# A graph-convolution and Mamba kernel: gate products moved to GpSimd, reductions joined, B's parts split elsewhere, weights loaded between the first rows, last pass on 128 partitions

## The chip, the cores and the metric

The kernel runs on one core of a Trainium2 chip. The core has TensorE (PE) for matmuls, VectorE (DVE), ScalarE (ACT) and GpSimd (POOL) for elementwise work, and SyncE (SP), whose queue issues most of the DMAs here. Each engine works through its own list of instructions in order and waits for others by semaphores. The metric is the time of one execution on the device, in microseconds (us), as the median of the runs.

## The reference, cut to what matters

The input `x` is 16 images of 96 channels and 64 x 64 pixels. A first layer builds a graph inside each 8 x 8 window and takes a maximum over edges; a second runs two Mamba layers over the 4096 pixels of an image and normalises over the whole batch.

```python
# layer 0
y = affine(conv1x1(x, fc1_w, fc1_b), fc1_s, fc1_t)
nodes = windows of 8 x 8 of y                      # 64 nodes of 96 channels
idx = top_k(-dist(nodes), 9)                       # nearest nodes, the node itself among them
feat = concat(x_i, x_j - x_i)                      # per edge, 192 values
h = gelu((einsum('bnkc,oc->bnko', feat, ew) + eb) * es + et)
h = max(h, over the 9 edges)                       # 192 channels
x = affine(conv1x1(h, fc2_w, fc2_b), fc2_s, fc2_t) + x
# layer 1, twice (D = 192 channels, 16 states)
xs, z = split(layernorm(seq) @ in_w)
xc = silu(causal_conv4(xs))
dt, Bm, Cm = split(xc @ xproj_w)                   # 6, 16, 16 columns
delta = softplus(dt @ dt_w + dt_b)
hstates = scan of h = exp(delta * A) * h + delta * Bm * xc
y = einsum(hstates, Cm) + Dp * xc
seq = seq + (y * silu(z)) @ out_w                  # the gate product
# then
out = fus_w @ concat(seq, relu(mean(x) @ gp_w))
out = batchnorm(out) * bn_g + bn_b + x
```

All inputs and outputs are float32.

## The kernel before, in words

**Tiling.** A *row* is 512 pixels (8 image rows, 8 windows) of one image: 128 rows. An *item* is a row in one of the two Mamba layers: 256 items, in the order image, layer, row. The 192 channels of Mamba lie on 128 partitions as 512 + 256 columns (the last 64 channels are folded over two halves), and in the scan as 128 partitions (two states of 64 channels each) by 3 groups by 512 pixels. So the 16 states of an item take 8 *steps*, and the loop has 2048 steps.

**The loop** (`for m, (n, p) in enumerate(order)`). In a step, VectorE scans `hb` from `da` and `db` (L861), then multiplies `u` by B's broadcast row into the next `db` (L707); in most items a small add (L852) carries the state over from the row before. PE makes the broadcast row from `bparts` with a 0/1 matrix (`bcast`, L702). ScalarE makes `da = exp(delta * A)` (L681) two steps ahead. GpSimd multiplies `hb` by C's rows `ct` (L887), which SyncE brings from DRAM (L674). One step later PE adds that product into `y` with `fold` (`folded`, L715 to L720). At step 1 of the next item VectorE multiplies `y`, in PSUM, into `z` (`gates`, two instructions issued at L850 or L854), and at step 6 `tail` projects the result (L740 to L745).

**Beside the steps** generators run, each advanced by one `yield` per step: `norm` and `prelude` for item n + 2 (they make `xc`, `z`, B, C, `delta`, `u`), `carry`, and layer 0 of a later row, one per two items: `nearest` (distances and the eight nearest, with `max` and `max_index` on VectorE) and `edges` (one-hot matrices, matmuls, Gelu into a `da` tile in groups of three, maxima over 8 edges). The maxima are queued: `later` holds them for two steps, `between` hands out at most one before the scan and one in steps 4 and 5 behind it, and `late` empties the rest. Yields marked TABLE keep `exp` away while another activation table is loaded. `apart`, `open_steps` and `close_steps` put a product at the end of a step and its use at the start of the next.

**B's parts.** bparts holds B three times in bfloat16, so that the three parts add up to float32. `xproj` yields B in three row groups; ScalarE casts all of them (L613) and casts a remainder again (L647), GpSimd subtracts twice over 512 columns (L640, L657).

**Head and end.** All weights are loaded and prepared first, mostly by ScalarE's queue (`compact`, `rows`, and the setup loop L195 to L254). Then `drain` runs `nearest` for rows 0 to 7 and `edges` for rows 0 to 5, one row's `nearest` beside the `edges` of the row before, then `norm` and `prelude` of items 0 and 1 one after another; the loop begins. The last pass (L908 to L918) waits for the statistics of all rows, reads `o_d` and `x1_d` in tiles of 96 x 2048, applies scale and shift, adds and writes.

Of the kernel before, what the change touches and what calls it, by code (L numbers as in the profile page):

```python
# [10 lines left out]
F32 = mybir.dt.float32  # L11
# [10 lines left out]
def tile_conv_knn_mamba(ctx: ExitStack, tc: tile.TileContext, w: dict, out: bass.AP):  # L22
# [85 lines left out]
    def compact(name, src):  # L108

        t = const.tile([128, 2], F32, name=name)  # L110
        src = src.rearrange("(p o) -> p o", o=1)
        nc.scalar.dma_start(out=t[:, 0:1], in_=src[:128])
        for h in range(2):
            nc.scalar.dma_start(out=t[h * CB : (h + 1) * CB, 1:2], in_=src[128:])
        return t

    def rows(name, src, n, pool=const):


        t = pool.tile([128, 3, n], F32, name=name)  # L120
        nc.vector.memset(t, 0.0)
        nc.scalar.dma_start(out=t[:, 0, :], in_=src[:128])
        for h in range(2):
            nc.scalar.dma_start(out=t[h * CB : (h + 1) * CB, 1 + h, :], in_=src[128:])
        return t
# [4 lines left out]
    e_b, e_s, e_t = (compact(f"e{k}", w[f"L0_conv_e{k}"]) for k in "bst")  # L130
    fc2T = rows("fc2T", w["L0_conv_fc2_w"], C)
# [28 lines left out]
    PARTS = (0, 64, 96)  # L160
    ONE0 = PARTS[2] + NS
# [14 lines left out]
    das = [const.tile([128, NB3, Q], F32, name=f"da{i}") for i in range(NDA)]  # L176
    zeros = const.tile([128, NB3], F32, name="zeros")
# [15 lines left out]
    conv_in, z_in, conv_b, xproj, dt_w, a_neg, dp_diag, out_w = ([] for _ in range(8))  # L193
    with tc.tile_pool(name="setup", bufs=2) as sp, tc.tile_pool(name="setup_ps", bufs=2, space=PSUM) as spp:
        for i in range(NL):  # L195


            iw = sp.tile([C, 2 * D], F32, tag="iw", name=f"in_w{i}")
            nc.scalar.dma_start(out=iw, in_=w["L1_conv_in_w"][i])
            g = sp.tile([C, 1], F32, tag="g", name=f"g{i}")  # L200
            nc.scalar.dma_start(out=g, in_=w["L1_conv_ln_g"][i].rearrange("(p o) -> p o", o=1))
            lb = sp.tile([C, C + 1], F32, tag="lb", name=f"lb{i}")
            nc.vector.memset(lb, 0.0)
            nc.scalar.dma_start(out=lb[:, C : C + 1], in_=w["L1_conv_ln_b"][i].rearrange("(p o) -> p o", o=1))
            gw = sp.tile([C, 2 * D], F32, tag="gw", name=f"gw{i}")
            nc.vector.tensor_scalar(gw, iw, g, None, ALU.mult)
            cm = sp.tile([C, C + 1], F32, tag="cm", name=f"cm{i}")
            nc.vector.memset(cm, 0.0)
            nc.vector.tensor_copy(cm[:, :C], cmat)
            pb = spp.tile([C + 1, 2 * D], F32, tag="pb", name=f"pb{i}")  # L210
            nc.tensor.matmul(pb, lhsT=cm, rhs=gw, start=True, stop=False)
            nc.tensor.matmul(pb, lhsT=lb, rhs=iw, start=False, stop=True)
            wz = const.tile([128, D], F32, name=f"z_in{i}")
            nc.vector.memset(wz, 0.0)
            nc.vector.tensor_copy(wz[: C + 1], pb[:, D:])
            z_in.append(wz)
            cw = sp.tile([C + 1, NT, D], F32, tag="cw", name=f"cw{i}")
            nc.scalar.dma_start(
                out=cw.rearrange("p k d -> p (k d)"),
                in_=w["L1_conv_conv_w"][i].rearrange("k d -> (k d)").unsqueeze(0).to_broadcast([C + 1, NT * D]),  # L220
            )
            wc = const.tile([128, NT, D], F32, name=f"conv_in{i}")
            nc.vector.memset(wc, 0.0)
            nc.vector.tensor_tensor(wc[: C + 1], cw, pb[:, :D].unsqueeze(1).to_broadcast([C + 1, NT, D]), ALU.mult)
            conv_in.append(wc)

            conv_b.append(compact(f"conv_b{i}", w["L1_conv_conv_b"][i]))
            xr = rows(f"xr{i}", w["L1_conv_xproj_w"][i], R + 2 * NS, sp)
            xp = const.tile([128, 3, ONE0], F32, name=f"xproj{i}")
            nc.vector.memset(xp, 0.0)  # L230
            for r, src, n in ((0, R, 2 * NS), (DT0, 0, R), (PARTS[1], R, NS), (PARTS[2], R, NS)):
                nc.vector.tensor_copy(xp[:, :, r : r + n], xr[:, :, src : src + n])
            xproj.append(xp)
            out_w.append(rows(f"out_w{i}", w["L1_conv_out_w"][i], C))
            dw = const.tile([128, D], F32, name=f"dt_w{i}")
            nc.vector.memset(dw, 0.0)
            nc.scalar.dma_start(out=dw[DT0 : DT0 + R], in_=w["L1_conv_dt_w"][i])
            nc.scalar.dma_start(out=dw[ONE0 : ONE0 + 1], in_=w["L1_conv_dt_b"][i].rearrange("(o d) -> o d", o=1))
            dt_w.append(dw)
            an = const.tile([128, NB3, NPR], F32, name=f"a{i}")  # L240
            for k in range(NB3):
                for h in range(2):
                    nc.scalar.dma_start(
# [136 lines left out]
    def most(out, g, at):  # L380

        nc.vector.tensor_reduce(out, g, AX.X, ALU.max)  # L382
        if at is not None:
            free.append(at)
# [560 lines left out]
```

## Time and profile before

| what | us |
|---|---|
| median of three runs (13182.12, 13199.09, 13199.22) | 13199.09 |
| span of the profiled execution | 13206.7 |
| first scan starts | 411.3 |
| last scan starts | 12927.6 |
| VectorE busy | 12215.5 (92%) |
| GpSimd busy | 11455.2 (87%) |
| PE busy | 11033.5 (84%) |
| ScalarE busy | 10512.7 (80%) |
| mean of a scan, of the product with C | 3.349, 3.452 |

The profile gives the time of the profiled execution as its span, from the first to the last instruction; what lies around it is not shown, and the median of the runs stands 7.6 us below that span. In the lines of the profile, a group has its line, engine, operation, tiles (out<-in) and shape, the count, then busy us, mean ns of one, and the idle time just before them with what ended it. A timeline line begins with start and duration in us. The duration of an instruction includes its filling and draining, which can overlap with a neighbour that does not depend on it.

### The profile page before, as it was taken

The numbers are of one execution on the slowest core, as the hardware profiler recorded it, in microseconds if no ns is written. First come the engines' busy times: TensorE is split into PE (matmuls) and PEld (weight loads), VectorE is DVE, ScalarE is ACT, GpSimd is POOL, SyncE is SP. The second block draws the span as 40 slices with busy tenths as digits, with TensorE's granted clock in tenths as the row PEclk, the third lists the DMA queues.
The fourth block names the chain that finished last, engine by engine and source line by source line (L and its number), as shares of the span: only waits on it lengthen the run. The fifth ranks groups of instructions, "written<-read, shape, count | busy, mean of one in ns | idle before, by whom it ended". The sixth has DMA issues, their size and how long they took to land.

```text
span 13206.7 us, 155165 instructions
## 1 busy us (share of the span) xinstructions
PE 11033.5 (84%) x46663; PEld 4408.0 (33%) x46664; DVE 12215.5 (92%) x9981; ACT 10512.7 (80%) x16401; POOL 11455.2 (87%) x7591
## 2 busy tenths in 40 slices
PE   6788888888888888888888888888888888888871
PEld 2233333333333333333333333333333333333320
DVE  2699999999999999999999999999999999999993
ACT  4688888888888888888888888888888888888762
POOL 1798999989999999999999899999999999998881
PEclk8899999999999999999999999999999999999985
DMA  1233333333333333333333333333333333333337
GB/s 27 72 86 91 91 91 86 92 91 86 92 88 93 87 90 94 89 88 91 91 90 87 91 92 87 90 92 91 85 94 89 90 88 90 93 88 90 84 89 237
DMA packets 887099, 1205.74 MB, mean 91 GB/s; under 512 B 282272, under 2 KB 413742, under 8 KB 877040
## 3 DMA queue, kind: packets, MB, share of 16 engines
q1 hardware_dynamic: 871792, 1169.34, 33.1%
q10 hardware_dynamic: 14464, 26.48, 0.6%
q8 instruction: 367, 6.01, 0.2%
q14 instruction: 476, 3.90, 0.1%
HBM read 706.82 MB, written 85.72 MB: 60 GB/s over the span
## 4 chain that ended last, share of the span: by engine, by line
DVE 30%; POOL 19%; PE 18%; ACT 14%; DMA 7%; issue 7%; SPq 4%; POOLq 0%; DVEq 0%; ACTq 0%
DVE hb L861 18%; POOL hb L887 12%; DVE db L707 9%; ACT da L681 5%; PE ya L718 3%; DMA ct<-cd 2%; SPq L663 2%; PE t L441 2%; PE t L438 1%; PE pj L584 1%; SPq L665 1%; PE yb L720 1%; PE bt L702 1%; PE pdta L622 1%; SPq L674 1%
## 5 line engine op out<-in xcount | busy, mean ns | idle before, releaser
L887 POOL TENSOR_TENSOR hb<-hb,ct 128x1536 f32<-128x1536 f32 x2048 | 7069.8, 3452 | 388.7 <-PE yb L720 87.9
L861 DVE TENSOR_TENSOR_SCAN hb<-da,db 128x1536 f32<-128x1536 f32 x2048 | 6859.6, 3349 | 108.3 <-ACT da L681 20.0
L681 ACT ACTIVATE da<-delta,a 128x511 f32<-128x511 f32 x6144 | 3940.0, 713 | 67.8 <-DVE hb L861 59.1
L707 DVE TENSOR_TENSOR db<-u,bt 128x1536 f32<-128x1536 f32 x2048 | 3602.9, 1759 | 170.0 <-PE pdtb L625 47.4
L718 PE MATMUL ya<-hb,fold 128*64 128x512 f32 x8192 | 2248.8, 628 | 220.9 <-POOL hb L887 215.2
L446 ACT ACTIVATE da<-t,eb,es 128x512 f32<-128x512 f32 x1536 | 1173.1, 777 | 778.9 <-PE t L438 518.7
L702 PE MATMUL bt<-bparts,bsel 128*128 128x512 bf16 x2047 | 797.5, 390 | 806.7 <-DVE db L707 745.8
L720 PE MATMUL yb<-hb,fold 128*64 128x256 f32 x8192 | 1265.6, 388 | 0.0
L720 PEld LDWEIGHTS yb<-hb,fold 128*64 128x64 f32 x8192 | 604.2, 141 | 1231.5 <-issue 1231.5
L438 PE MATMUL t<-oh,vu 128*128 128x512 f32 x2048 | 993.2, 607 | 23.3 <-ACT da L446 23.3
L584 PE MATMUL pj<-hn,conv_in 128*128 128x512 f32 x2048 | 930.9, 597 | 9.8 <-POOL hn L567 9.8
L718 PEld LDWEIGHTS ya<-hb,fold 128*64 128x64 f32 x8192 | 491.0, 139 | 1313.9 <-issue 552.2
L404 POOL TENSOR_SCALAR oh<-idb,node 64x1024 f32<-64x1024 uint16 x256 | 731.2, 2856 | 131.1 <-DMA idb<-idxd 131.1
L886 POOL COPY state<-hb 128x3 f32<-128x3 f32 x1792 | 342.1, 191 | 571.7 <-DVE hb L861 428.1
L441 PE MATMUL t<-oh,vu 128*64 128x512 f32 x2048 | 572.1, 638 | 302.1 <-ACT da L446 299.0
L382 DVE TENSOR_REDUCE hqa<-da 128x64 f32<-128x512 f32 x1024 | 677.0, 671 | 149.2 <-ACT da L446 149.1
L415 PE MATMUL pv<-ewT,y 96*64 96x192 f32 x2048 | 458.9, 349 | 248.6 <-ACT rs L564 166.0
L438 PEld LDWEIGHTS t<-oh,vu 128*128 128x128 f32 x2048 | 395.7, 195 | 465.3 <-issue 265.9
L596 ACT ACTIVATE xc<-pj,conv_b 128x512 f32<-128x512 f32 (+1 forms) x512 | 297.6, 581 | 289.6 <-PE pj L589 183.6
L584 PEld LDWEIGHTS pj<-hn,conv_in 128*128 128x128 f32 x2048 | 395.7, 193 | 395.0 <-issue 374.5
L589 PE MATMUL pj<-hn,conv_in 128*64 128x256 f32 x4096 | 498.9, 385 | 0.0
L415 PEld LDWEIGHTS pv<-ewT,y 96*64 96x64 f32 x2048 | 246.2, 140 | 696.9 <-ACT rs L564 268.6
(188 smaller groups left out, 18447.0 us busy)
## 6 DMA issues: line engine op xcount, KB each, us to landing
ct<-cd SPq DMA_DIRECT2D x4096, 128.0 KB
delta<-ln SPq DMA_DIRECT2D x1024, 128.0 KB
u<-s SPq DMA_DIRECT2D x1024, 128.0 KB
idb<-idxd SPq DMA_DIRECT2D x256, 256.0 KB
delta<-ln SPq DMA_DIRECT2D x1024, 64.0 KB
u<-s SPq DMA_DIRECT2D x1024, 64.0 KB
x<-in_x SPq DMA_DIRECT2D x128, 192.0 KB
rn<-r4d SPq DMA_DIRECT2D x128, 192.0 KB
```

The lines of the kernel that those rows point to most:

```text
L404: nc.gpsimd.tensor_scalar(ohj, numbers, node, None, ALU.is_equal)
L438: nc.tensor.matmul(t, lhsT=vus[p][:, part, :128], rhs=ohw[part], start=True, stop=True)
L441: nc.tensor.matmul(t[half(h)], lhsT=vus[p][:, h, 128:], rhs=ohw[h], start=True, stop=True)
L446: nc.scalar.activation(g, t, AF.Gelu, bias=e_b[:, j : j + 1], scale=e_s[:, j : j + 1])
L584: nc.tensor.matmul(ps, lhsT=wt[:, t, :128], rhs=hn[:, off : off + Q], start=(t == 0), stop=(t == taps - 1))
L681: nc.scalar.activation(da[:, c, 1:Q], delta[:, c, 1:], AF.Exp, scale=a_neg[i][:, c, p : p + 1])
L702: nc.tensor.matmul(bt, lhsT=bsel[:, p, :], rhs=made[n][2], start=True, stop=True)
L707: nc.vector.tensor_tensor(db, made[n][5], bt.unsqueeze(1).to_broadcast([128, NB3, Q]), ALU.mult)
L718: nc.tensor.matmul(y[0][half(h)], lhsT=fold, rhs=hb[:, h, :], start=False, stop=(p == NPR - 1))
L720: nc.tensor.matmul(y[1][half(h)], lhsT=fold, rhs=hb[:, 2, bass.ts(h, QH)], start=False, stop=(p == NPR - 1))
L861: nc.vector.tensor_tensor_scan(*(t.rearrange("p c q -> p (c q)") for t in (hb, das[at], db)), 0.0, ALU.mult, ALU.add)
L887: nc.gpsimd.tensor_tensor(hb, hb, ct.unsqueeze(1).to_broadcast([128, NB3, Q]), ALU.mult)
```

## The change

- **Gates.** `gates` goes. In step 1 ScalarE copies `y` (now one tile of two PSUM banks) to SBUF (`emptied`), and GpSimd multiplies the copy by `z` (`gate`) behind its product with C. `z` and the copies come from four fixed tiles `zs`.
- **Maxima.** The three reductions of a `da` tile become one over 128 x 1536, and the two `tensor_tensor` maxima one over 128 x 768; `hq` and `sa` have a new layout, and the fc2 product reads it with four matmuls and one for the residual in place of four.
- **B's parts.** `xproj` yields B once. A DMA spreads the 16 x 512 rows over 128 x 64, GpSimd makes three bfloat16 parts of 64 columns, and three DMAs put them into `bparts`.
- **Head.** The Mamba weights are loaded by SyncE in a generator `weights`, advanced once per turn of `drain`. Before the loop only rows 0 to 4 get `nearest` and rows 0 to 2 `edges`, with the preludes of items 0 and 1 beside them. The loop takes the other rows, rows 4 to 7 at two or three yields per step, rows 8 to 13 at other steps than before, later rows as before.
- **Last pass.** Tiles of 128 x 3072, three channels' pieces per partition; scale and shift are spread to that layout through DRAM.
- **Smaller.** `o` is written into its `seq` tile; `taken` frees a `da` tile when none is free; `ahead` may run in a held step when no `da` is ready.

```diff
-    PARTS = (0, 64, 96)
-    ONE0 = PARTS[2] + NS
+    PARTS = (0, 32, 64)
+    ONE0 = DT0 + R
...
+    zs = deque(const.tile([128, Q + QH], F32, name=f"z{i}") for i in range(4))
...
+    def weights():
+        made_of = []
+        for i in range(NL):
+            big, small = (das[2 * i + at].rearrange("p c q -> p (c q)") for at in range(2))
+            iw = big[:C, : 2 * D]
+            nc.sync.dma_start(out=iw, in_=w["L1_conv_in_w"][i])
...
+            cw = big[: C + 1, 4 * D :].rearrange("p (k d) -> p k d", d=D)
+            nc.sync.dma_start(
+                out=cw.rearrange("p k d -> p (k d)"),
+                in_=w["L1_conv_conv_w"][i].rearrange("k d -> (k d)").unsqueeze(0).to_broadcast([C + 1, NT * D]),
+            )
+            yield
+            conv_b.append(compact(f"conv_b{i}", w["L1_conv_conv_b"][i], nc.sync))
+            yield
...
     def most(out, g, at):
-        nc.vector.tensor_reduce(out, g, AX.X, ALU.max)
-        if at is not None:
-            free.append(at)
+        nc.vector.tensor_reduce(out(), g.rearrange("p s (i k) -> p s i k", k=KO), AX.X, ALU.max)
+        free.append(at)
...
-        late.append(partial(nc.vector.tensor_tensor, hqa, hqa, sa, ALU.max))
-        late.append(partial(nc.vector.tensor_tensor, hqb, hqb, sb, ALU.max))
+        late.append(lambda: nc.vector.tensor_tensor(maxima[0], maxima[0], sa, ALU.max))
...
         nc.scalar.copy(dbl[:ONE0], ps)
-        nc.scalar.copy(bp[:ONE0], ps)
         yield
+        bs = pr.tile([128, QS], F32, tag="bs", name=f"bs_{nm}", bufs=1)
+        nc.sync.dma_start(out=bs, in_=dbl[:NS, :])
...
-        nc.gpsimd.tensor_tensor(dbl[PARTS[1] : ONE0], dbl[PARTS[1] : ONE0], bp[PARTS[1] : ONE0], ALU.subtract)
+        b3 = pr.tile([128, 3, QS], BF16, tag="b3", name=f"b3_{nm}")
+        for part in range(3):
+            nc.gpsimd.tensor_copy(b3[:, part], bs)
+            if part < 2:
+                nc.gpsimd.tensor_tensor(bs, bs, b3[:, part], ALU.subtract)
         yield
+        bp = bparts[n % 2]
+        for r, part in zip(PARTS, range(3)):
+            nc.sync.dma_start(out=bp[r : r + NS], in_=b3[:, part])
...
-        nc.scalar.copy(bp[PARTS[1] : ONE0], dbl[PARTS[1] : ONE0])
...
-        nc.gpsimd.tensor_tensor(bp[PARTS[2] : ONE0], dbl[PARTS[2] : ONE0], bp[PARTS[2] : ONE0], ALU.subtract)
...
-    def gates(n, y):
...
+    def emptied(n, y):
+        yc = zs.popleft()
+        nc.scalar.copy(yc, y.rearrange("p s q -> p (s q)")[:, : Q + QH])
+        return yc
+
+    def gate(n, yc):
+        z = made[n][1]
+        nc.gpsimd.tensor_tensor(yc, yc, z, ALU.mult)
+        zs.append(z)
+        gated[n] = yc
...
+    FIRST = 3
     drain(nearest(0, 0))
-    for q in range(NQ):
-        drain(*([nearest(0, q + 1)] if q + 1 < NQ else []), *([edges(0, q)] if q < NQ - 2 else []))
-    for n in range(2):
-        drain(norm(n))
-        drain(prelude(n))
+    for q in range(FIRST):
+        drain(nearest(0, q + 1), edges(0, q), *([prepared(q - 1)] if q else []))
+    drain(nearest(0, FIRST + 1))
...
+    for r in range(FIRST + 1, NB * NQ):
+        pace = 1 if r >= NQ else 2
+        at = NPR * (r - FIRST) - 3 if r < NQ else max(16 * (r - NQ) + 29, 14 * (r - NQ) + 41)
+        rows_at.setdefault(at, []).append((edges, r, 2 * pace - 1))
+        if r > FIRST + 1:
+            rows_at.setdefault(at - 16 // pace - pace + 1, []).append((nearest, r, pace))
...
-        acts = opening + (gates(n - 1, y) if p == 1 and n else [])
+        acts = list(opening)
...
+        if p == 1 and n:
+            yc = emptied(n - 1, y)
...
         nc.gpsimd.tensor_tensor(hb, hb, ct.unsqueeze(1).to_broadcast([128, NB3, Q]), ALU.mult)
+        if p == 1 and n:
+            gate(n - 1, yc)
...
+            o = pn.tile([128, NJ, 1024], F32, tag="o", name=f"bo_{b}")
+            nc.sync.dma_start(out=o.rearrange("p j f -> p (j f)"), in_=flat(o_d[b]))
```

## The prediction

> **What bounds the kernel now.** I read the page first (busy shares, slices, costliest groups), then three stages by windows, VectorE's groups, the timelines of VectorE and GpSimd around 7000 us, and the packets of the last stage.
>
> ```profile
> 0.00:411.30 411.30, 248.47 (x771) 95.03 (x773) 89.99 (x254) 179.54 (x241) 82.62 (x80) 0.80 0.12 27
> 436.00:12927.60 12491.60, 10773.10 (x45861) 4309.29 (x45861) 12031.96 (x9683) 10256.01 (x16114) 11357.31 (x7504) 0.98 0.33 89
> 12950.00:13206.70 256.70, 0.00 (x0) 0.00 (x0) 73.24 (x32) 66.95 (x32) 0.00 (x0) 0.50 0.97 291
> ```
>
> The columns are stage, length, busy us of PE, weight load, VectorE, ScalarE, GpSimd, then clock, DMA share, GB/s. The head is 411 us in which no engine is two thirds busy: a chain of latencies. The loop is 94% of the time, with VectorE busy 96%, GpSimd 91%, PE 86%, ScalarE 82%. The last pass is DMA: 0.97 busy at 291 GB/s.
>
> ```profile
> 7018.90 1.76 DVE L707 TENSOR_TENSOR db<-u,bt 128x1536 f32<-128x1536 f32 x1
> 7020.77 0.17 DVE L852 TENSOR_TENSOR db<-db,first 128x3 f32<-128x3 f32 x1
> 7020.85 0.68 DVE L382 TENSOR_REDUCE hqa<-da 128x64 f32<-128x512 f32 x1
> 7021.44 3.34 DVE L861 TENSOR_TENSOR_SCAN hb<-da,db 128x1536 f32<-128x1536 f32 x1
> 7024.70 0.66 DVE L382 TENSOR_REDUCE hqa<-da 128x64 f32<-128x512 f32 x1
> 7025.28 1.75 DVE L707 TENSOR_TENSOR db<-u,bt 128x1536 f32<-128x1536 f32 x1
> ```
>
> Start to start, a step without extras (scans at 7009.89 and 7015.44) is 5.55 us: scan 3.46, product 1.80, the small add 0.30. The part beyond the instructions is the wait of each for the one before it. An independent reduction fills that gap: between scan and product it adds 3.84 - 3.46 = 0.38 us, not its 0.66. So durations mislead here; I price by scan-to-scan distances.
>
> ```profile
> L850 DVE TENSOR_TENSOR z<-z,ya 128x512 f32<-128x512 f32 x135 | 92.8, 687 | 147.7 <-PE ya L718 146.1
> L382 DVE TENSOR_REDUCE hqa<-da 128x64 f32<-128x512 f32 x1024 | 677.0, 671 | 149.2 <-ACT da L446 149.1
> L859 DVE TENSOR_TENSOR hqa<-hqa,sa 128x512 f32<-128x512 f32 x122 | 105.3, 863 | 0.0
> L652 POOL TENSOR_TENSOR s<-ln,xc 128x768 f32<-128x768 f32 x256 | 467.6, 1827 | 0.2
> L640 POOL TENSOR_TENSOR dbl<-dbl,bparts 48x512 f32<-48x512 f32 x256 | 295.9, 1156 | 47.8 <-PE pdtb L625 27.6
> L657 POOL TENSOR_TENSOR bparts<-dbl,bparts 16x512 bf16<-16x512 f32 x256 | 297.0, 1160 | 20.1 <-POOL first L690 0.2
> ```
>
> The gates also make VectorE wait for the last fold (146 us); the 149 us before the reductions lie in the head (none in a window over the loop). One layer-0 row falls to every two items, so I count in pairs: medians of scan distances are 48.6 (even item) + 49.5 (odd) = 98.1 us, of which 16 bare steps are 88.8.
>
> **Gates to GpSimd.** Steps that hold gates last 7.49 and 6.32 (medians), against 5.55: VectorE wins 1.94 + 0.77 = 2.71 per pair. ScalarE gains a PSUM copy of 128x768: between 128x512 from PSUM (0.59) and 128x768 from SBUF (0.84), about 0.80. GpSimd gains one 128x768 product at 1.82, 1.78 net of the overlap with its neighbour. It stands after the product of step 1; in step 1 the folds into the single y tile now wait for ScalarE's copy instead of VectorE. In the timeline that fold ran at 7007.92 after ScalarE's L564 anyway, so about 0.8 us later, and the next broadcast (7010.85) has 2.1 us to spare. Behind the copy on ScalarE stands L564, hence the norm; behind GpSimd's product stand hn, which PE's projections wait for, and the products whose folds PE waits for in order.
> The Trainium skill (GPSIMD Engine Reference, Engine selection) keeps two-input elementwise work on VectorE because GpSimd is about twice as slow. The rows agree in kind (1.82 against 0.69 + 0.41). By that rule alone the move costs 0.7 per item, 184 us, instead of winning; it decides only if GpSimd is the bound.
>
> **B's parts.** ScalarE loses two casts (0.58, 0.61): with the copy, minus 0.4 per item. GpSimd loses 1.16 + 1.16 (about 2.4 with gaps), and gains three copies and two subtractions of 128x64. Not in the trace. Each lies between a 128x3 copy (0.19) and a 48x512 subtraction (1.16), so 1.3 to 6.2 for the five with 0.08 gaps. They are nearest to the 128x24 product (0.23); forty columns more at 2.1 ns (128x1536 against 128x768) make 0.3, with gaps 1.9. The far end would make GpSimd the bound and belongs to the slower rival. SyncE issues four more DMAs per item at about 0.6, 2.4 us on a queue that issues some 21 of 49 us. They are asked for in prelude steps 4 and 7; the matmul that reads them is five steps, 27 us, later. No cost, unless the queue is held by the first of them waiting for ScalarE's dbl, where the DMA of C waits already.
>
> **Joined maxima.** Twelve reductions per pair become four of 128x1536. By scan distances the twelve and the two maxima cost 2.30 + 4.06 = 6.36 per pair, since ten stand in gaps. An element takes 1.07 ns (the gates: 0.687 for 512, 0.413 for 256), so a reduction of 1536 lasts 0.67 + 1.10 = 1.77, adds 1.68 back to back and 1.48 in a gap. Four: 5.9; one joined maximum 0.75: 6.65. So the join earns nothing: +0.3. Ends: -1.3 by plain durations (12 x 0.67 + 1.28 against 8.0), +1.2 if none of the four finds a gap.
> The Trainium skill (VectorE: DVE Perf Modes, the TRN2 errata) says the fixed cost sits between instructions and one large tile pays it once. By it eight fewer instructions of 0.12 fixed (0.67 less 512 x 1.07 ns) would give 1.0 per pair, about 125 us. The row at 7024.70 shows the fixed part already filled.
>
> **The loop's sum.** VectorE: 98.1 - 2.71 + 0.3 = 95.7 per pair. GpSimd's work per step up to its product of that step, medians: even 6.0, 5.7, 6.7, 7.1, 5.5, 5.0, 4.9, 6.7; odd 5.0, 5.7, 6.7, 5.5, 5.5, 5.0, 3.6, 6.7 = 91.3. New: step 0 +0.7, step 2 +1.8, step 5 -1.2 in both items: 94. Below VectorE, but bunched. Lag, by which a GpSimd product starts after its scan's end, is the lag of the step before, plus GpSimd's work, minus VectorE's step, and not under 0.3. For before this gives 0.3, 1.5, 3.0, 2.7 in even steps 1 to 4; measured 0.34, 1.46, 3.23, 2.69. For after, with steps of 5.55 and two of 7.0: even 2.7, 5.7, 7.5, 6.0, then down to 2.2; odd 3.6, 6.5, 6.3, 6.1, down to 0.3. What lag is free? The product of B two steps on needs the broadcast, which PE issues behind this fold: two steps (11.1) - 3.45 - 1.6 fold - 0.6 leaves 5.4, or 6.9 to 8.3 where slow reductions stand in those steps. Only odd step 2 is over, by 0.9 to 1.1. With 0.3 for spread (the worst tenth lags 0.9 more than the median), the pair is 96.9: -1.2. Over 119 pairs -143; the 14 items after the last row lose 0.7 each, -10. Bounds: 95.7 (-286 over 119 pairs), and 98.1 if lag eats all.
>
> **Head.** Row loads (L312) start at 48.9, 76.4, 118.8, 162.0 ... 330.2: 27 us for the first row, 42 for a row with the edges of the one before, 27 for the last, 54 for two preludes. After the change only rows 0 to 4 and edges 0 to 2 come first. The first load stands on SyncE behind 16 DMAs (7 us) and the broadcast of conv weights, 13.16 us in the chain of waits: matmul at 25 instead of 51.9. Then 27 for row 0; the other weights, 46 us on ScalarE's queue before and now between the first rows' own DMAs on SyncE, of which I take 20 exposed (ends 0, 46); 42 for row 1; two rows with a prelude beside them, 55 each (42 if hidden, 69 if not); 27 for row 4; 9 to the scan. Sum 260, -151 (214 to 314). In exchange the first 36 steps carry 4.8 edges and 3 nearest. ScalarE per row: 22.9 and 1.7; per item without rows (10256 - 122 x 24.6)/256 = 28.3. That is 242 us; before they took 232. At 91% occupancy 265: +33 (+10 at full, +63 at the loop's 82%). Rows 8 to 13 start at other steps of an item than now; I leave that to these ends.
>
> **Last pass.** 75.5 MB. Packets of 8 KB fall into groups: 309 ns for a quarter of the loads, a median of 511 for the rest. The fastest on all 16 engines is 424 GB/s, 178 us; at 291 it is 259. I take it that 128 partitions in place of 96 even out the groups, which no run here shows, so the fast end, plus about 30 for filling, a tail of tiles twice as large and the trip of gain and shift through DRAM: 208 of 260, -52 (0 to -70).
>
> **Nothing else.** The fc2 product has eight short passes for six mixed (+0.2 us a row, on PE's idle 14%); writing o into its seq tile holds that tile one DMA longer of a ring of 13; the narrower xproj, taken() and the held rule touch no wait that the trace shows.
>
> **Sum.** -151 + 33 - 143 - 10 - 52 = -323. The span profiled is 13206.7, 7.6 above the median of three; 12884 against it, 12875 against the median.
>
> **Rivals.** *GpSimd takes the win*: the lag is not free, pairs stay at 98.1. For it: 94 of work with gaps in 96.9. Against: lag to 3.2 costs VectorE nothing now. 180 faster, 13020. *Slower*: PE's in-order folds wait for the late products (0.59 at 7025.53 already), so that broadcasts, Gelu matmuls and ScalarE slip; the tolerated lag is then only what is seen today, 4.1 in the worst tenth. Peaks of 7.5 and 6.5 cost 3.4 + 2.4 less what each wait gives back, pairs of about 100.6: +298, 13310. It decides from pairs over 99.6. *All ends good*: pairs 95.7, head 214, first steps +10, last pass -70: -553, 12645. *The last pass or the head does not move* belongs to the ranges above.
>
> **How the numbers follow.** Forecast 0.52 (its own range 12790 to 12960), GpSimd takes the win 0.23, all good 0.13, slower 0.09, no change 0.03. 0.2% (26 us) is about what a measurement tells. Faster 0.88, same 0.03, slower 0.09. From 12690 (half of the good case) to 13070 (past the second): about 0.1 is outside on each side.
>
> **What would show it.** First scan near 260; scan distances 5.55 in steps 0 and 1; lags of 6 to 7 us around steps 2 to 4 with VectorE idle on bt under 1 us; reductions near 1.77 us; last pass above 360 GB/s. Wrong, if VectorE waits on bt several us per pair, GpSimd passes 97% busy, or the reductions take under 1.3.

## The result and the profile after

The changed kernel takes 13314.1 us (13307.5 to 13318.2) beside 13197.7 for the kernel before: a ratio of 1.0088, with a 95% interval of 1.0076 to 1.0101. It is slower by 116 us where 323 less was forecast. Its profiled execution has a span of 13314.3 us, 107.6 longer than that of before.

The first view is that of windows over the whole of the changed kernel; columns as in the view of before (length, busy us of PE, weight load, VectorE, ScalarE, GpSimd, then clock, DMA share, GB/s). The stages are the head, items 0 to 15, items 16 to 255, and what follows the last scan.

```profile
0.00:261.60 261.60, 147.56 (x477) 57.64 (x477) 45.81 (x116) 107.94 (x148) 65.53 (x94) 0.82 0.17 36
261.60:1283.80 1022.20, 828.95 (x3179) 321.11 (x3179) 779.60 (x550) 769.91 (x1138) 750.58 (x548) 0.88 0.27 72
1283.80:13107.70 11823.90, 10273.93 (x43235) 3977.74 (x43236) 11254.63 (x7580) 9498.71 (x14870) 10793.42 (x8001) 0.96 0.34 90
13107.70:13314.30 206.60, 11.29 (x34) 3.66 (x30) 62.91 (x26) 60.36 (x54) 6.64 (x3) 0.53 0.88 367
```

The head and the last pass went as forecast or better: the first scan at 261.6 for 411.3, and the end part moves 367 GB/s, where from the last scan on the kernel before moved 272. The second line is the surprise: the first 16 items take 1022 us, where before they took 796 with VectorE busy 752 of them. Here VectorE is busy 780 of 1022. Stage by stage the 107.6 us are:

| stage | before | after | difference |
| --- | --- | --- | --- |
| to the first scan | 411.3 | 261.6 | -149.7 |
| items 0 to 15 | 796.1 | 1022.2 | +226.1 |
| items 16 to 239, per pair of items | 98.11 | 99.06 | +0.95, 112 pairs: +105.9 |
| items 240 to the last scan | 731.9 | 729.7 | -2.2 |
| last scan to the end | 279.1 | 206.6 | -72.5 |

Five groups of instructions over the whole changed kernel, of VectorE, GpSimd and ScalarE (busy us, mean ns of one, then the idle time before them and its releasers):

```profile
L734 DVE TENSOR_TENSOR db<-u,bt 128x1536 f32<-128x1536 f32 x2048 | 3607.3, 1761 | 487.8 <-PE bt L729 345.1 <-DMA ct<-cd 8.2 <-DVE hb L914 2.3
L413 DVE TENSOR_REDUCE hq<-da 128x192 f32<-128x1536 f32 x512 | 890.3, 1739 | 104.1 <-ACT da L476 103.8 <-issue 0.2
L507 DVE TENSOR_TENSOR hq<-hq,sa 128x768 f32<-128x768 f32 x128 | 320.6, 2505 | 0.2
L759 POOL TENSOR_TENSOR z<-z,z 128x768 f32<-128x768 f32 x256 | 466.4, 1822 | 2.6 <-ACT z L754 2.6
L754 ACT COPY z<-y 128x768 f32<-128x768 f32 x256 | 198.5, 775 | 9.0 <-PE y L747 9.0
```

The gates are gone from VectorE, the joined reduction lasts 1.74 us, the gate on GpSimd 1.82, the copy 0.78: the sizes that were forecast. Two rows are not: the product waits 345 us for the broadcast, and the joined maximum lasts 2.5 us where 0.75 was priced.

The timeline of VectorE in the changed kernel, the same place in a pair as the lines shown of before (start, us, instruction):

```profile
7007.93 1.74 DVE L413 TENSOR_REDUCE hq<-da 128x192 f32<-128x1536 f32 x1
7009.59 3.34 DVE L914 TENSOR_TENSOR_SCAN hb<-da,db 128x1536 f32<-128x1536 f32 x1
7013.03 1.76 DVE L734 TENSOR_TENSOR db<-u,bt 128x1536 f32<-128x1536 f32 x1
7014.83 0.17 DVE L905 TENSOR_TENSOR db<-db,first 128x3 f32<-128x3 f32 x1
7014.91 2.63 DVE L507 TENSOR_TENSOR hq<-hq,sa 128x768 f32<-128x768 f32 x1
7017.47 3.34 DVE L914 TENSOR_TENSOR_SCAN hb<-da,db 128x1536 f32<-128x1536 f32 x1
```

And GpSimd's in the same stretch:

```profile
7008.11 3.46 POOL L939 TENSOR_TENSOR hb<-hb,ct 128x1536 f32<-128x1536 f32 x1
...
7013.27 3.46 POOL L939 TENSOR_TENSOR hb<-hb,ct 128x1536 f32<-128x1536 f32 x1
```

GpSimd's product ends at 7016.73, the maximum at 7017.54, 0.81 later. Of the 128 maxima on that line 121 start while such a product runs, and 120 of those end 0.81 to 0.82 us after it, whatever they lasted. The other seven took 0.94 to 0.96. So the maximum is not slow, it is held. The reduction at 7007.93 runs beside the product of 7008.11 and isn't held, nor are the scans, nor the product beside them (3.46): the reduction and the scan read one operand from SBUF (the scan's db is in PSUM), the maximum reads two.

### The profile page after: what moved, and what is told of

It is laid out like the page before. It is cut to its first block, busy times and chain, and to the rows that moved or that the text cites. A ratio compares the mean times of both kernels' runs of the same rounds, so it can differ in the third digit from the quotient of the medians.

```text
span 13314.3 us, 155658 instructions
## 1 busy us (share of the span) xinstructions
PE 11261.7 (85%) x46920; PEld 4360.1 (33%) x46920; DVE 12142.9 (91%) x8270; ACT 10436.9 (78%) x16209; POOL 11616.2 (87%) x8644
## 4 chain that ended last, share of the span: by engine, by line
DVE 26%; POOL 24%; PE 14%; ACT 12%; issue 10%; DMA 4%; SPq 4%; POOLq 0%; DVEq 0%; ACTq 0%
DVE hb L914 16%; POOL hb L939 14%; DVE db L734 9%; ACT da L708 4%; PE y L745 2%; SPq L690 2%; POOL ln L674 2%; DMA ct<-cd 1%; SPq L692 1%; POOL e L672 1%; PE y L747 1%; POOL hn L591 1%; POOL ln L676 1%; PE bt L729 1%; SPq L701 1%
## 5 line engine op out<-in xcount | busy, mean ns | idle before, releaser
L708 ACT ACTIVATE da<-delta,a 128x511 f32<-128x511 f32 x6144 | 3937.3, 713 | 22.3 <-DVE hb L914 17.8
L745 PE MATMUL y<-hb,fold 128*64 128x512 f32 x8192 | 2287.1, 638 | 260.8 <-POOL hb L939 252.3
L476 ACT ACTIVATE da<-t,eb,es 128x512 f32<-128x512 f32 x1536 | 1172.9, 776 | 723.6 <-PE t L468 449.3
L747 PE MATMUL y<-hb,fold 128*64 128x256 f32 x8192 | 1270.1, 389 | 0.0
L747 PEld LDWEIGHTS y<-hb,fold 128*64 128x64 f32 x8192 | 608.4, 142 | 1256.6 <-issue 1256.1
L413 DVE TENSOR_REDUCE hq<-da 128x192 f32<-128x1536 f32 x512 | 890.3, 1739 | 104.1 <-ACT da L476 103.8
L745 PEld LDWEIGHTS y<-hb,fold 128*64 128x64 f32 x8192 | 495.2, 141 | 1319.9 <-issue 563.1
L620 ACT ACTIVATE xc<-pj,conv_b 128x512 f32<-128x512 f32 (+1 forms) x512 | 297.2, 580 | 570.0 <-PE pj L613 448.7
L613 PE MATMUL pj<-hn,conv_in 128*64 128x256 f32 x4096 | 525.6, 400 | 1.8 <-ACT xc L620 1.5
L742 PE MATMUL y<-xc,dp_diag 128*128 128x512 f32 x512 | 370.6, 815 | 152.6 <-ACT z L754 152.6
```

The source lines that it names most:

```text
L413: nc.vector.tensor_reduce(out(), g.rearrange("p s (i k) -> p s i k", k=KO), AX.X, ALU.max)
L476: nc.scalar.activation(g, t, AF.Gelu, bias=e_b[:, j : j + 1], scale=e_s[:, j : j + 1])
L708: nc.scalar.activation(da[:, c, 1:Q], delta[:, c, 1:], AF.Exp, scale=a_neg[i][:, c, p : p + 1])
L745: nc.tensor.matmul(y[half(h), 0], lhsT=fold, rhs=hb[:, h, :], start=False, stop=(p == NPR - 1))
L747: nc.tensor.matmul(y[half(h), 1, :QH], lhsT=fold, rhs=hb[:, 2, bass.ts(h, QH)], start=False, stop=(p == NPR - 1))
```

## The theories and the runs

Four theories were set against one another. *Held maximum*: joining the maxima put a two-operand VectorE instruction where GpSimd's product is running, about 1.67 us per row. *Early rows*: rows 3 to 13, moved into the first 16 items, cost there what the stage view shows. *Late products*: the prediction's slower rival, GpSimd's lag delays folds and broadcasts. *ScalarE's order*: the new copy of y delays what PE waits for. The table is measured from each run's trace; "wait" is VectorE's wait for bt per pair in items 16 to 239. The kernel before was run again beside each group of these runs, with medians of 13194.2 to 13202.8; the ratios below are to those.

| kernel | time, us | first scan | items 0-15 | pair | wait | end part |
| --- | --- | --- | --- | --- | --- | --- |
| before | 13197.7 | 411.3 | 796.1 | 98.11 | 0.11 | 279.1 |
| changed | 13314.1 | 261.6 | 1022.2 | 99.06 | 1.90 | 206.6 |
| a_max_early | 13157.8 | 261.0 | 1011.3 | 97.76 | 2.20 | 205.6 |
| a_rows_first | 13231.1 | 387.5 | 806.4 | 99.11 | 1.95 | 205.4 |
| a_gates_back | 13493.5 | 260.3 | 1003.0 | 100.75 | 0.15 | 205.2 |
| b_joined | 13472.6 | 409.7 | 815.4 | 100.28 | 0.13 | 279.8 |
| a_split | 13193.0 | 261.7 | 1033.4 | 97.92 | 2.50 | 205.9 |
| a_gate_late | 13288.4 | 260.7 | 1011.4 | 98.90 | 1.73 | 209.7 |
| a_first4 | 13212.2 | 302.1 | 881.6 | 99.16 | 1.98 | 206.2 |
| b_last | 13143.7 | 407.8 | 792.5 | 98.40 | 0.15 | 204.4 |
| a_copy_between | 13290.3 | 260.4 | 1018.6 | 98.90 | 1.54 | 206.3 |
| b_gates | 13355.6 | 407.2 | 807.9 | 99.40 | 2.71 | 284.6 |
| best_joined | 12992.8 | 305.0 | 874.3 | 97.19 | 1.49 | 206.2 |
| best_split | 13028.2 | 299.4 | 868.3 | 97.44 | 1.67 | 206.3 |

### The joined maximum

**a_max_early**, the changed kernel with the maximum behind the scan:

```diff
-        while late:
-            ...
         hb = pr.tile(...)
         nc.vector.tensor_tensor_scan(...)
         free.append(at)
+        while late:
+            ...
```

> The changed kernel with one move: the joined maximum is issued right behind the scan and not right ahead of the next one, so that it starts before GpSimd's product of the step. Held maximum (the maximum waits for GpSimd's product, 2.62 us where 0.95 would do): the maximum falls to about 0.95 us, 1.7 us per row less, 122 rows: 13314 - 205 = about 13110, and GpSimd's product of that step starts about 0.6 us later. Late products (the time is lost to GpSimd's lag, and VectorE's win is handed back as a wait for the broadcast): the maximum falls as well, but VectorE's wait on bt grows from 1.9 to 3 or more us per pair, about 13290.

It took 13157.8 us, 0.9969 of before (0.9958 to 0.9980): 156 less than the changed kernel. Its timeline, VectorE and then GpSimd:

```profile
5954.13 3.35 DVE L909 TENSOR_TENSOR_SCAN hb<-da,db 128x1536 f32<-128x1536 f32 x1
5957.40 0.93 DVE L507 TENSOR_TENSOR hq<-hq,sa 128x768 f32<-128x768 f32 x1
5958.25 1.75 DVE L734 TENSOR_TENSOR db<-u,bt 128x1536 f32<-128x1536 f32 x1
```

```profile
5952.06 3.46 POOL L939 TENSOR_TENSOR hb<-hb,ct 128x1536 f32<-128x1536 f32 x1 [2.96 <-PE pj L608]
5957.62 4.03 POOL L939 TENSOR_TENSOR hb<-hb,ct 128x1536 f32<-128x1536 f32 x1 [2.10 <-DVE hb L909]
```

Now the maximum starts first and lasts 0.93, and it is GpSimd's product that is held: 4.03 for 3.46. The steps around it confirm it: the step that held the maximum fell from 7.86 to 5.55, the step it moved to rose from 5.54 to 6.21. The gain is 50 short of the forecast, since the pair is 1.29 shorter and not 1.64, as these two steps would make it; VectorE's wait for bt is 0.3 longer. The rival's signs (a wait of 3 or more, 13290) did not come. The Trainium skill (SBUF — State Buffer, "SBUF: two separate sides") says that a VectorE instruction with two SBUF inputs and a GpSimd instruction that reads SBUF exclude each other for the whole of the one that starts first. Both directions are in these rows, with 2.63 for 0.93 and 4.03 for 3.46.

**b_joined**, the kernel before with the joins alone:

```diff
-                    later[1].append(partial(most, hqb4[:, w2] if part == 2 else hqa4[:, 2 * w2 + part], ...))
+                later[1].append(partial(most, hq[:, 2 * hf + p], g3.rearrange("p s (i k) -> p s i k", k=KO), at))
...
-        late.append(partial(nc.vector.tensor_tensor, hqa, hqa, sa, ALU.max))
-        late.append(partial(nc.vector.tensor_tensor, hqb, hqb, sb, ALU.max))
+        late.append(partial(nc.vector.tensor_tensor, hq, hq, sa, ALU.max))
```

> The kernel before with the joined reductions and the joined maximum alone (gates, B's parts, head and last pass as before). The prediction's term: +0.3 us per pair, 13200 + 36 = about 13235. The rule of the Trainium skill that one large tile pays the fixed cost once: -1.0 per pair, about 13075. Held maximum: the joined maximum stands against GpSimd's product here too and lasts 2 to 2.6 us, +1.9 to 2.2 us per pair, 13430 to 13460.

It took 13472.6 us, 1.0208 (1.0191 to 1.0225), with pairs of 100.28, 2.17 above before. The groups of VectorE in b_joined:

```profile
L382 DVE TENSOR_REDUCE hq<-da 128x192 f32<-128x1536 f32 x512 | 891.0, 1740 | 175.2 <-ACT da L442 174.8 <-issue 0.4
L847 DVE TENSOR_TENSOR hq<-hq,sa 128x768 f32<-128x768 f32 x122 | 322.2, 2641 | 0.0
```

So the join by itself costs 2% of this kernel, and neither the prediction's +0.3 came true nor the -1.0 that followed from the rule weighed there (the Trainium skill, VectorE: DVE Perf Modes, the TRN2 errata: one large tile pays the fixed cost once). With the 2.64 measured in place of the 0.75 that was priced, the prediction's own sum gives 0.3 + 1.89 = 2.19. In the kernel before, 73 of the 122 maxima of 128x512 start during a product too, but late in it: in the step that holds them four reductions run ahead of them, so that they start 4.1 us behind the scan and last 0.86 for 0.68 undisturbed. In b_joined nothing of layer 0 stands ahead of the joined one in its step; it starts 2.0 us behind the scan, and all 122 are held.

**a_split** undoes the join in the changed kernel (twelve reductions of 128x512, two maxima):

```diff
-                later[1].append(partial(most, partial(maximum, 2 * hf + p), g3, at))
+                    last = at if part == 2 else None
+                    later[1].append(partial(most, partial(maximum, 2 * hf + p, part), g, last))
...
-        late.append(lambda: nc.vector.tensor_tensor(maxima[0], maxima[0], sa, ALU.max))
+        for parts in (slice(0, 2), slice(2, 3)):
+            late.append(lambda q=parts: nc.vector.tensor_tensor(maxima[0][:, :, q], ...))
```

> The changed kernel with the reductions and the maxima split as before (twelve of 128x512, maxima of 128x512 and 128x256), all else as changed. Held maximum, and joining worth nothing: three reductions stand ahead of the maxima again, GpSimd's product is over by then, and the 2.17 us per pair that the join alone cost come back: pairs 96.9, 13314 - 2.17 x 119 = about 13055. If the join is held back by something that only the changed kernel has (the gates' lag), it differs from 2.17 by more than 0.5: under 13000 or over 13115.

13193.0 us, 0.9993 (0.9983 to 1.0002): the changed kernel without the join is as fast as the kernel before, and not faster. Pairs fell by 1.14, not by 2.17, which is a miss by more than the 0.5 allowed: beside the gates on GpSimd part of what the join cost returns as waiting for bt, 2.50 per pair for 1.90.

### The first items

**a_rows_first** does six rows of edges ahead of the loop again and starts every later row at the steps of before:

```diff
-    FIRST = 3
+    FIRST = 6
...
-        pace = 1 if r >= NQ else 2
-        at = NPR * (r - FIRST) - 3 if r < NQ else max(16 * (r - NQ) + 29, 14 * (r - NQ) + 41)
+        pace = 1
+        at = 16 * (r - NQ) + 29
```

> The changed kernel with six rows of edges ahead of the loop again, and the later rows started at the steps of before (weights still loaded between the rows, all else as changed). Early rows (rows 3 to 13 inside the first 16 items cost 225 us there, not 33): first scan at 262 + 3 x 42 = 388, items 0 to 15 back from 1022 to about 800, together 13314 + 126 - 222 = about 13220. Other cause (the first items are slow for the gates or for late products, not for the rows): items 0 to 15 stay near 1000 and the time rises to about 13420.

13231.1 us, 1.0024 (1.0014 to 1.0034); first scan at 387.5 (388 forecast) and items 0 to 15 in 806 (about 800). The gates and the joins stayed, so the 216 us are the rows'; 126 of them are paid again in the head, and 83 are gained. VectorE's two waiting groups over items 0 to 15, first of the changed kernel, then of a_rows_first:

```profile
L914 DVE TENSOR_TENSOR_SCAN hb<-da,db 128x1536 f32<-128x1536 f32 x128 | 428.8, 3350 | 87.9 <-ACT da L708 80.5 <-POOL e L672 1.0 <-ACT da L476 0.5
L734 DVE TENSOR_TENSOR db<-u,bt 128x1536 f32<-128x1536 f32 x128 | 225.4, 1761 | 140.0 <-PE bt L729 126.2 <-DMA ct<-cd 7.3 <-DMA cd<-dbl 0.4
```

```profile
L914 DVE TENSOR_TENSOR_SCAN hb<-da,db 128x1536 f32<-128x1536 f32 x128 | 428.9, 3351 | 8.3
L734 DVE TENSOR_TENSOR db<-u,bt 128x1536 f32<-128x1536 f32 x128 | 225.5, 1762 | 39.0 <-PE bt L729 30.7
```

**a_first4** tells pace from place: four rows ahead, rows 4 to 7 at the faster pace, and every row from the eighth on at step 5 of an odd item, as before.

```diff
-    FIRST = 3
+    FIRST = 4
...
-        at = NPR * (r - FIRST) - 3 if r < NQ else max(16 * (r - NQ) + 29, 14 * (r - NQ) + 41)
+        at = NPR * (r - FIRST) - 3 if r < NQ else 16 * (r - NQ) + 29
```

> The changed kernel with four rows ahead of the loop, rows 4 to 7 in the first four items at the faster pace, and every row from the eighth on started at step 5 of an odd item, as before. The step at which a row starts: items 4 to 15 come back to 49.5 each (from 58.6 on average) and only items 0 to 3 stay near 75, so 894 for the first 16; first scan at 304; 13314 + 42 - 128 = about 13230. The number of rows alone (a row costs the same wherever it starts): items 4 to 8 and 11 to 15 stay near 60, 13300 or more.

13212.2 us, 1.0012 (1.0003 to 1.0022). Items 0 to 3 lasted 79.7, 75.0, 75.0 and 59.5, and items 4 to 15 average 49.4, where the changed kernel has 57.5 to 74.8 for all but two of items 4 to 15. So of the 226 us 97 lie in items 0 to 3, where the early rows run at the faster pace, and 129 lie behind them; 125 of those go with the step at which rows 8 to 13 start. What that does is seen in ScalarE's table loads of items 0 to 15 (L476 is the Gelu of a row, L620 the Silu of a prelude, L708 and L719 are Exps), changed kernel and then a_first4:

```profile
L476 ACT ACT_TABLE_LOAD x41 | 52.6, 1283 | 0.7
...
L620 ACT ACT_TABLE_LOAD x20 | 25.7, 1283 | 0.3
...
L708 ACT ACT_TABLE_LOAD x9 | 11.5, 1283 | 0.1
L719 ACT ACT_TABLE_LOAD x8 | 10.3, 1283 | 0.1
```

```profile
L476 ACT ACT_TABLE_LOAD x27 | 34.6, 1283 | 0.5
...
L620 ACT ACT_TABLE_LOAD x16 | 20.5, 1283 | 0.3
...
L708 ACT ACT_TABLE_LOAD x4 | 5.1, 1283 | 0.1
L719 ACT ACT_TABLE_LOAD x3 | 3.8, 1283 | 0.1
```

Each change of table costs 1.28 us: 120 loads in the first 16 items of the changed kernel, 86 in a_first4. In items 4 to 15 they are 78 and 48. There a_first4 loads the Gelu table once for the six Gelus of half a row; at the other steps the two groups of three come apart, and Exps and a Silu stand between them, each with its own load. ScalarE in item 8 of the changed kernel:

```profile
840.07 0.78 ACT L476 ACTIVATE da<-t,eb,es 128x512 f32<-128x512 f32 x1 [0.24 <-PE t L471]
840.87 1.28 ACT L708 ACT_TABLE_LOAD   x1
842.16 1.94 ACT L708 ACTIVATE da<-delta,a 128x511 f32<-128x511 f32 x3
844.12 1.28 ACT L620 ACT_TABLE_LOAD   x1
845.42 0.69 ACT L620 ACTIVATE xc<-pj,conv_b 128x512 f32<-128x512 f32 x1
846.12 1.28 ACT L476 ACT_TABLE_LOAD   x1
847.42 1.45 ACT L476 ACTIVATE da<-t,eb,es 128x512 f32<-128x512 f32 x2
```

The 30 loads more are 38 us of ScalarE. What reaches VectorE are waits: in items 4 to 15 it waits 62 us ahead of its scans and 70 ahead of its products, in a_first4 0.3 and 9, and the difference is 123 of the 125. How the loads, the late Exps and PE's queue share those waits was not separated.

### The gates

**a_gates_back** puts the gate products back on VectorE:

```diff
-        acts = list(opening)
+        acts = opening + (gates(n - 1, y) if p == 1 and n else [])
...
-            yc = emptied(n - 1, y)
...
-            gate(n - 1, yc)
```

> The changed kernel with the gate products on VectorE again, from PSUM, at their old place; the copy of y and GpSimd's product are gone. Late products: without the gate's 1.8 us GpSimd's lag after step 2 shrinks, VectorE's wait on bt falls from 1.9 to about 0.1 us per pair and with it what hangs on it; pairs go under 98.1 and the time to 13200 or less. Held maximum: the gates cost VectorE 2.7 us per pair and the wait on bt gives back at most 1.8, pairs near 100.0, about 13410.

13493.5 us, 1.0226 (1.0209 to 1.0243); pairs of 100.75. The gates on GpSimd are worth 1.70 us per pair in this kernel, near the forecast of 2.71 less 1.2. The two steps that hold them last 7.57 and 6.98 here and 5.53 without, 3.5 together (0.8 over the kernel before: VectorE waits 1.93 us per pair ahead of the gates for 1.31, probably because y is now one tile), and the wait for bt takes 1.75 back.

**b_gates** does the same to the kernel before, where B's parts are still large:

```diff
-        acts = opening + (gates(n - 1, y) if p == 1 and n else [])
+        acts = list(opening)
...
+        if p == 1 and n:
+            yc = emptied(n - 1, y)
...
+        if p == 1 and n:
+            gate(n - 1, yc)
```

> The kernel before with the gate products on GpSimd alone (ScalarE's copy of y, four z tiles), all else as before. Additive parts: what undoing them cost in the changed kernel, 1.70 us per pair, is won here: pairs 96.4, 13197 - 1.7 x 119 - 8 = about 12985. The prediction's term: -2.71 + 1.2 of lag, about 13010. If GpSimd, which here still has the large B parts (2.4 us per item), becomes the bound: pairs of 98 or more, 13200 or above.

13355.6 us, 1.0117 (1.0100 to 1.0134): slower, and a miss for the additive theory. The groups of VectorE in b_gates:

```profile
L709 DVE TENSOR_TENSOR db<-u,bt 128x1536 f32<-128x1536 f32 x2048 | 3604.2, 1760 | 473.8 <-PE bt L704 328.9 <-PE pdtb L627 48.3 <-DVE hb L869 2.7
L867 DVE TENSOR_TENSOR hqa<-hqa,sa 128x512 f32<-128x512 f32 x122 | 237.8, 1949 | 0.0
```

The last row is the same instruction that took 863 in the kernel before. GpSimd's product at that step starts 1.97 us behind its scan (median) for 0.76 before, and so it is still running when 106 of the 122 maxima come, for 73 before. From 98.11 the pair loses 2.71 of gates and gains 2.6 in waits for bt, 0.4 in waits for first and 1.1 in held maxima: 99.5, measured 99.40. By its number the third expectation fits, but GpSimd is busy 93% of items 16 to 239 here and 94% in best_joined: it is not full, its products come late. a_split, which has the gates with the short B's parts, lies at 97.92, 1.48 less: 1.0 of that is the maximum (943 ns for 1949) and 0.4 the waits for bt and first. So the gates pay only where GpSimd's products come early enough. That the B's parts make them early is likely (1.3 us of GpSimd per item for 2.3), but no run has them alone, and a_split also has the smaller edits.

**a_gate_late** issues GpSimd's gate behind the product of step 3:

```diff
-        if p == 1 and n:
+        if p == 3 and n:
             gate(n - 1, yc)
```

> The changed kernel with GpSimd's gate product issued behind the product of step 3 and not of step 1; ScalarE's copy stays at step 1. If the 1.9 us per pair that VectorE waits for bt is the gate's 1.8 us in GpSimd's lag at steps 2 and 3 (the tolerated lag of the prediction, 5.4): the lags of even steps 2 and 3 fall from 5.1 and 5.6 to about 3.5, the wait on bt to 0.5 or less, pairs to 97.7, 13314 - 160 = about 13155. If the wait comes from B's parts or from PE's own order: the wait stays near 1.9 and the time near 13314.

13288.4 us, 1.0069 (1.0052 to 1.0086). The lags of even steps 2 and 3 fell from 5.11 and 5.64 to 3.34 and 4.01, as meant, and the wait for bt only from 1.90 to 1.73. So it is not mainly this lag that VectorE pays for, and late products fall as the main cause. The time itself says little: its interval overlaps that of the changed kernel (1.0076 to 1.0101). The place of the wait is even step 2 (1.33 of 1.90). PE there in the changed kernel, and then ScalarE:

```profile
5742.99 0.33 PE L453 MATMUL pv<-ewd,y 96*64 96x192 f32 x1
5745.56 1.07 PE L356 MATMUL ss<-sq,ones_cc 96*96 96x512 f32 x2 [2.24 <-POOL state L938]
5746.46 1.81 PE L742 MATMUL y<-xc,dp_diag 128*128 128x512 f32 x2
...
5750.94 0.39 PE L729 MATMUL bt<-bparts,bsel 128*128 128x512 bf16 x1
```

```profile
5742.22 1.93 ACT L708 ACTIVATE da<-delta,a 128x511 f32<-128x511 f32 x3
5744.05 0.77 ACT L754 COPY z<-y 128x768 f32<-128x768 f32 x1
5744.73 0.68 ACT L588 ACTIVATE rs<-pvar,eps_t 96x512 f32<-96x512 f32 x1
```

PE stands 2.24 us before a matmul of the next row. The profile names GpSimd as the releaser here and ScalarE's L588 in 70 of the 112 such waits of items 16 to 239; but in all 112 the matmul starts 0.14 to 0.15 us after the end of L588. sq was ready at 5738.2; the matmul's PSUM buffer is freed when L588, the Ln of the norm, has read it, here at 5745.4, and L588 stands behind the new copy. Folds and the broadcast queue behind that matmul. The copy is not all of this wait: with the gates back on VectorE and no copy (a_gates_back) PE still stands 1.52 us per pair there, for 2.23, and VectorE waits only 0.15 for bt.

**a_copy_between** issues the copy behind that Ln:

```diff
         nc.scalar.activation(rs, ps, AF.Ln, bias=eps_t[:C], scale=1.0 / C)
+        while emptying:
+            emptying.pop()()
...
-            yc = emptied(n - 1, y)
+            emptying.append(lambda n=n, y=y: copies.append(emptied(n - 1, y)))
```

> The changed kernel with ScalarE's copy of y issued behind the Ln of the next norm and not ahead of it. ScalarE's order: in even step 2 PE stands 2.24 us before the ss matmul of the next row, for the PSUM buffer that the Ln frees, and the Ln stands behind the copy (0.77); folds and the broadcast queue behind that matmul. Then the wait on bt in even step 2 falls from 1.33 to about 0.7 us per pair and the time to 13314 - 75 = about 13240. GpSimd's lag is the cause after all: the wait stays at 1.3 and the time within 25 us of 13314.

13290.3 us, 1.0066 (1.0049 to 1.0083). At its place the reading holds: the wait in even step 2 fell from 1.33 to 0.45. But 0.60 more appeared in odd step 2 (0.08 to 0.68) and 0.25 before the small add in even step 7, so only 24 us came off, and the interval again overlaps that of the changed kernel. The wait was moved, not removed; what holds the rest of it stays open.

### The last pass, and the edits together

**b_last** is the kernel before with the last pass of the changed one, and nothing else.

```diff
-    F = L // 2
-    with tc.tile_pool(name="bn", bufs=3) as pn:
+    NJ = C * L // (128 * 1024)
+    ...
+    with tc.tile_pool(name="bn", bufs=5) as pn:
```

> The kernel before with the last pass on 128 partitions alone. The prediction's term: -52 (0 to -70), 13148. What the changed kernel shows from its last scan to the end: 206.6 for 279.1, -72, 13128. If that gain came from elsewhere (o written into its own tile, the earlier parts): less than 40, over 13160.

13143.7 us, 0.9955 (0.9938 to 0.9972). The windows view of its end:

```profile
12953.00:13158.00 205.00, 12.01 (x36) 3.94 (x36) 64.39 (x30) 60.15 (x54) 5.33 (x2) 0.53 0.88 370
```

Its end part is 204.4 for 279.1, so the new last pass alone gives the whole of the 72 us. Its tiles differ in three things, 128 partitions for 96, 12 KB per partition for 8 and five buffers for three. Which of them does it was not separated, but the packets point to the first two: those of 12 KB take 460 ns, nine in ten of them within 10 ns, where of the loads of 8 KB in the kernel before a quarter take 309 and the others 526 (median). 309 for 8 KB and 460 for 12 KB are the same 26.5 to 26.7 bytes per ns. By the medians 51 are seen; this run's loop was 0.3 us per pair longer, and runs of it spread from 13126 to 13160.

**best_joined** puts a_max_early, a_first4, a_gate_late and a_copy_between into one kernel (no new lines). **best_split** is that with a_split in place of a_max_early; the kernel that its expectation calls the fourth is best_joined.

> The changed kernel with four edits together: maximum behind the scan (-156 measured), four rows ahead and the old start steps (-102 measured), gate product behind step 3 (-26 measured), copy behind the Ln (-75 expected). If they add up: 13314 - 359 = 12955. If the two that shorten PE's wait on one another's account are the same gain: about 13030.

> As the fourth kernel, but with the reductions and maxima split as before (-121 measured) in place of the joined maximum behind the scan (-156). If they add up: 12990. Held maximum only: the split one has no held maximum and its reductions fill gaps, so once PE's waits are gone it should be the shorter by up to 0.5 us per pair, 12930.

best_joined took 12992.8 us, 0.9838 of before (0.9822 to 0.9855), and best_split 13028.2, 0.9871 (0.9855 to 0.9888). Both beat both kernels. Both are 38 us over the sum, which took the copy at the 75 expected; with its measured 24 the sums are 13006 and 13041, and both kernels are 13 under them. That the split one would be the shorter did not come true: its wait for bt (1.67 for 1.49) and for first (0.56 for 0.13) is longer. It has held maxima as well, 58 of 124 start during a product, and they last 1.01 us on average for 0.68. The groups of best_joined:

```profile
L737 DVE TENSOR_TENSOR db<-u,bt 128x1536 f32<-128x1536 f32 x2048 | 3606.8, 1761 | 361.3 <-PE bt L732 234.7 <-DMA ct<-cd 6.3 <-DVE hb L913 3.2
L507 DVE TENSOR_TENSOR hq<-hq,sa 128x768 f32<-128x768 f32 x128 | 122.1, 954 | 0.1
```

The maximum is down to 0.95 us. The 235 us for bt, 1.5 per pair in the steady stage, are what is left of it; where they could go without coming back elsewhere was not tried.

## Why the prediction was wrong

Between the 323 us forecast to be won and the 107.6 lost in the profiled executions lie about 430. With the -143 and -10 shared out over the items, 200 of them are in items 0 to 15, 240 in items 16 to 239, 9 behind those and 1 in the head, and 20 the other way in the last pass.

- **Head: right.** 260 and -151 were forecast, 261.6 and -149.7 came out, and a row with edges cost 42 (three more rows in a_rows_first: 125.9).
- **First items: wrong, by 193 us.** The step that failed is "That is 242 us; before they took 232. At 91% occupancy 265: +33 ... Rows 8 to 13 start at other steps of an item than now; I leave that to these ends." It priced the rows by ScalarE's busy time. The 36 steps took 337 and not 265: ScalarE was busy 263 of them and not 242, at 78% and not at 91%. The steps behind them up to item 15, for which nothing was set down, took 120 more than before. a_first4 shows that there it is the step at which a row starts, and most of the loss is waiting: in the first 16 items VectorE waits 80 us for da and 126 for bt, where before it was 20 and 5.
- **Joined maxima: wrong.** The failing step is "one joined maximum 0.75: 6.65. So the join earns nothing: +0.3." It is 2.5, held, and the join costs 2.17 per pair alone and 1.14 beside the gates. The row quoted in the prediction already said so: the maximum of 128x512 took 863 ns where a gate of the same size took 687. The gate reads one operand from PSUM. Joining also took away the short reductions that ran ahead of the maximum while GpSimd finished.
- **Gates: the effect nearly right, its cost put in the wrong place.** Steps 0 and 1 went to 5.53 to 5.56, which is 2.74 per pair for the 2.71 forecast. "Only odd step 2 is over, by 0.9 to 1.1" failed: the wait is in even step 2 and it is 1.8 more per pair, though GpSimd lagged less than forecast (5.6 at most for 7.5); a_gate_late shows that this lag is not its main cause. The prediction saw that the norm stands behind the copy on ScalarE, but gave the broadcast "2.1 us to spare" without following the PSUM buffer that the norm frees to the matmul in front of it. That this buffer is the whole cause is not shown: a_copy_between moved the wait to other steps.
- **Pairs.** 96.9 forecast, 99.06 measured: of the 2.16, 0.84 is the join (1.14 for 0.3) and 1.3 the rest (a_split's 97.92 for 96.6), which its waits account for: those for bt and first are together 2.6 longer than before, and 1.2 was allowed.
- **Last pass: right, its start misplaced.** -52 with an end of -70 was forecast, -72 came out (b_last alone: -75 in its end part). The 208 us forecast for it are near the 206.6 measured; but from the last scan the kernel before takes 279.1, and the 260 of the sum count from 22 us later. That 128 partitions even out the groups of packets fits the packets after (460 ns for nearly all), though the larger packets came with them. The 511 ns quoted is the median of all loads; that of the slower ones is 526.
- **The rivals.** The slower one gave 13310, and 13314 was measured, but not for its reason: pairs are 99.06 and not 100.6, below the 99.6 from which it would decide, and late products are not mainly what they wait for. With the held maximum and a part of the first items taken out, the two costs that the prediction had not priced, and two smaller moves, the change's parts make the faster kernel, as best_joined shows.

## What to carry to other kernels

Before two instructions are joined, look at what the other engines do at the moment when the joined one starts: short pieces ahead of it may have been its shield, and a row that is slower than its equal in size (863 for 687) is the sign to look for. Work that is moved into a loop is priced by what it does to the loop's order at its place, table changes and queue positions, and not only by the busy time it adds. When an instruction is put into a queue, follow each buffer that the instructions behind it free, one engine further than the first wait.

## What the runs showed of the hardware

- A VectorE maximum with both inputs in SBUF that starts during a GpSimd product ends 0.81 to 0.82 us after that product, in 120 of 121 cases; started first, it lasts 0.93 and the product 4.03 for 3.46. Reductions (one SBUF input) and scans (one input in SBUF, one in PSUM) beside the same product kept their 1.74 and 3.35.
- From the last scan to the end, with filling and tail, 76 MB moved at 272 GB/s in tiles of 96 partitions by 8 KB and at 367 to 370 in tiles of 128 by 12 KB.
- Casts and subtractions of 128x64 on GpSimd last 0.24 and 0.30 us, the product of 128x768 1.82.
- A change of ScalarE's table took 1.28 us in the loop, whichever function it was for, and the next instruction began 12 ns after it (median).
